# The last image's 3x3 convolution in a four-layer network: four output columns from six transformed parts, in blocks of 16 rows

## The chip, the cores and the metric

The kernel is one program on one core of a Trainium2 chip. The metric is the device time of one execution in microseconds, as the median of several runs. A profiled execution, which the hardware profiler records, is longer than the others; its own time and span stand in the table below.

## The reference

Four images of 256 channels and 64x64 pixels, in fp32, go through four layers, each of the form x = x + layer(groupnorm(x)). Layer 0 is a deformable convolution with a feed-forward part, layer 1 a linear attention with 5x5 depthwise convolutions, layer 3 an attention against a pooled image. The change is in layer 2, a 3x3 convolution with weights reduced to their sign times a scale for each output channel:

```python
def _L2_conv_ref(x, weights):                      # x: groupnorm of the image, 256 x 64 x 64
    real_w = weights.reshape(256, 256, 3, 3)
    scale = mean(abs(real_w), axis=(1, 2, 3), keepdims=True)
    bin_no_grad = scale * sign(real_w)
    clipped = clip(real_w, -1.0, 1.0)
    bin_w = (bin_no_grad - clipped) + clipped
    return conv2d(x, bin_w, stride=1, padding=1)
...
x = x + _L2_conv_ref(_gn(x), L2_conv_weights)      # 32 groups of 8 channels
x = x + _L3_conv_ref(_gn(x), ...)
```

## The kernel before

Channels lie on the 128 partitions in KT = 2 halves, pixels along the free dimension. The four images are staged one behind the other, and each stage runs the gathers of one image (`sample`, indirect DMAs issued by POOL) beside later layers of earlier images. Each layer is a generator that yields costs; `beside` (in `run`) advances several generators in proportion, so that their instructions interleave. Within `with ordered():` the order so emitted is the order on TensorE, VectorE (DVE), ScalarE (ACT) and GpSimd (POOL). The last call of `beside`, for the last image's layer 2 and the rest of the third image's layer 3 (`rest`), stands outside `ordered`; there the framework's scheduler decides the order of each engine from its own estimates, and that order is fixed in the program.

`binarise` runs once, beside the second image's `sample`, within the first fifth of it. It makes the weights' signs and scales and transforms each row of three taps into four, which `w2_d` holds in DRAM; its share of the interleaving is planned from the constant `BINARY`, 62.

`layer2` works in NB = 8 blocks of 8 rows. `normed` loads ten padded rows (`xp`, on the SP queue) and normalises them on ACT (L1048). `parts` makes, from each group of four neighbouring columns, four parts of two output columns (L1036; on POOL for the last two images, where `self.alone` is set, on DVE before). For each output half m and each pair of parts, twelve matmuls with 256 columns (two parts, two input halves, three row taps, L1085) sum into one PSUM bank. `leave` (L1061 on) adds the bank to the block's pixels `xv`: the first pair is the output columns themselves (L1065), the second a shared sum and difference (L1067 to L1069). The statistics of layer 3's groupnorm (`stats`, L110) and the store to `x5_d` (L1072) follow. `leave` is called through the list `before`, during the matmuls of the next bank; banks of the last image come from `long`, which cycles through the tags `acc` and `dp`. The next block's `normed` and `parts` are called in the middle of the current block.

At the start of the last stage, the last image's layer 1 ends (its matmuls to L943, its store at L954). The four attention steps of a block in the third image's layer 3 are each scores (L1185), maximum (L1186), exp (L1191), transpose (L1197) with its copy (L1199), and product (L1203); a block ends with L1213. After the last image's layer 2, only its layer 3 is left (`pooled(N - 1, True)`).

```python
CONV, SECOND = NB * 22.5 + 11, 568
...
beside(range(STEPS), STEPS, (conv(N - 1, "right"), CONV, 0, 1), (rest, 150, 0, 1))
```

Of the kernel before, what the change touches and what calls it, by code (L numbers as in the profile page):

```python
# [9 lines left out]
F32 = mybir.dt.float32  # L10
I32 = mybir.dt.int32
AF = mybir.ActivationFunctionType
ALU = mybir.AluOpType
# [4 lines left out]
P = 128  # L18
N, C, H, W = 4, 256, 64, 64
HW = H * W  # L20
KT = C // P
NB = HW // 512
# [4 lines left out]
NCH = NT // CT  # L27
# [9 lines left out]

CONVOLVE, OFFSETS, BINARY = NB * 9 + 26, 60, 62  # L40
FEED = NB * 40 + 8
LINEAR, LAST = 938, 624
STEPS = 900
CONV, SECOND = NB * 22.5 + 11, 568
EPS_BN = 1e-5
EPS_GN = 1e-5
EPS_ATT = 1e-5
# [24 lines left out]
class Net:  # L72
# [131 lines left out]
    def setup(self):  # L204
        nc, cp, a = self.nc, self.cp, self.a
# [38 lines left out]
        dt = self.dp.tile  # L244
# [5 lines left out]

        self.s_d = [dt([HW * PT, G * 5], F32, name=f"sd{n}") for n in im]
        self.w2_d = dt([P, KT, 3, 4, C], F32, name="w2")

    def binarise(self):


        nc = self.nc
        parts = [(k, slice(t, t + 3)) for k in range(KT) for t in range(0, 9, 3)]
        with self.tc.tile_pool(name="bin", bufs=1, side="left") as sp, \
                self.tc.tile_pool(name="bin2", bufs=2, side="left") as bp:  # L260

            def real(part):
                k, t = part
                w = bp.tile([P, 3, C], F32, name="w")
                nc.sync.dma_start(w, self.a["w2T"][:, k, t])
                return w

            sums = sp.tile([P, 6, C], F32, name="sums")
            for i, part in enumerate(parts):
                w = real(part)  # L270
                yield 1
                t = bp.tile([P, 3, C], F32, name="t")
                nc.vector.scalar_tensor_tensor(t, w, -1.0, w, ALU.mult, ALU.max)
                nc.vector.tensor_reduce(sums[:, i], t.rearrange("p t o -> p o t"), AX.X, ALU.add)
                yield 2
            ps = self.ps()
            for i in range(6):
                nc.tensor.matmul(ps[:, 0:C], self.ones, sums[:, i], start=i == 0, stop=i == 5)
            scale = sp.tile([P, C], F32, name="scale")
            nc.scalar.activation(scale, ps[:, 0:C], AF.Copy, scale=1.0 / (C * 9))  # L280
            yield 2
            for part in parts:
                w = real(part)
                yield 1
                t = bp.tile([P, 3, C], F32, name="t")
                s = bp.tile([P, 3, C], F32, name="s")
                nc.vector.tensor_scalar(t, w, 0.0, None, ALU.is_lt)
                nc.vector.scalar_tensor_tensor(s, w, 0.0, t, ALU.is_gt, ALU.subtract)
                nc.vector.tensor_tensor(s, s, scale.unsqueeze(1).to_broadcast([P, 3, C]), ALU.mult)
                yield 3  # L290
                nc.vector.tensor_scalar(t, w, -1.0, 1.0, ALU.max, ALU.min)
                nc.vector.tensor_tensor(s, s, t, ALU.subtract)
                nc.vector.tensor_tensor(s, s, t, ALU.add)
                yield 2
                u = bp.tile([P, 4, C], F32, name="u")
                nc.scalar.copy(u[:, 0], s[:, 0])
                nc.scalar.activation(u[:, 1], s[:, 2], AF.Copy, scale=-1.0)
                nc.scalar.activation(t[:, 0], s[:, 1], AF.Copy, scale=0.5)
                nc.vector.tensor_tensor(t[:, 1], s[:, 0], s[:, 2], ALU.add)
                for e, op in ((2, ALU.add), (3, ALU.subtract)):  # L300
                    nc.vector.scalar_tensor_tensor(u[:, e], t[:, 1], 0.5, t[:, 0], ALU.mult, op)
                nc.sync.dma_start(self.w2_d[:, part[0], part[1].start // 3], u)
                yield 2


# [791 lines left out]
            before.pop()()  # L1097


    def layer3(self, n, st, wide=False):  # L1100
        nc, tc, a = self.nc, self.tc, self.a
        M = HW // 4
        with tc.tile_pool(name=f"na{n}", bufs=1, side="left") as sp, \
# [17 lines left out]
            ps = self.ps()  # L1121
# [96 lines left out]
    def run(self):  # L1218
# [15 lines left out]
        def beside(steps, number, *works):  # L1234


            spent, open_ = [0] * len(works), set(range(len(works)))

            def advance(share):
                for j in sorted(open_):  # L1240
                    work, total, lo, hi = works[j]
                    while j in open_ and lo <= share and spent[j] < total * (share - lo) / (hi - lo) or share >= hi:
                        cost = next(work, None)
                        if cost is None:
                            open_.discard(j)
                        if not cost:
                            break
                        spent[j] += cost

            for i, _ in enumerate(steps, 1):  # L1250
                advance(i / number)
            while any(works[j][3] <= 1 for j in open_):
                advance(1)
# [28 lines left out]
        with ordered():  # L1282
            beside(range(STEPS), STEPS, (feed(N - 1), FEED, 0, 0.27), (linear(N - 1), LAST, 0.27, 1), (rest, SECOND, 0.27, 1.05))
        self.spare = False
        beside(range(STEPS), STEPS, (conv(N - 1, "right"), CONV, 0, 1), (rest, 150, 0, 1))

        self.banks = cycle(["mm", "mm", "mm", "vk"])
        for _ in pooled(N - 1, True):
# [95 lines left out]
```

## Time and profile before

| what | value |
|---|---|
| time, median of 3 runs | 7713.78 us (7711.9 to 7732.44) |
| profiled execution, own time | 8695.07 us |
| span of the profiled execution | 8693.3 us |
| mean granted TensorE clock | 0.803 |
| busy over the span: PE, PE weight load | 5880.0 us (68%), 3498.6 us (40%) |
| busy over the span: DVE, ACT, POOL | 4817.7 us (55%), 3541.0 us (41%), 4934.7 us (57%) |
| first and last gather issued by POOL | 137.1 us, 7190.2 us |
| last image's layer 2: first record of L1085, last one's start | 8306.88 us, 8481.8 us |

"Busy" is the time in which an engine executes; PE is TensorE's matmuls, "PE weight load" its loads of stationary operands, which overlap matmuls. A line such as `L1085 PE MATMUL ps<-xd,w` is the code's line, the engine, the operation and its output and inputs by the program's names. Every matmul in fp32 appears as two records. In lists in order of time, the first number is the start in microseconds from the span's start and the second a length; what stands in brackets is the idle time before it and what ended it.

### The profile page before, as it was taken

The page shows a single profiled execution, that of the slowest core. Times are in us where ns is not written, and L with a number is a line of the kernel's source. Part 1 is how long each engine was busy: PE and PEld are TensorE (multiplying, and loading weights), DVE is VectorE, ACT ScalarE, POOL GpSimd, SP SyncE. Part 2 cuts the span into 40 slices and gives each one's busy share as a digit, 9 for nine tenths or more (in the row PEclk, how much of TensorE's full clock was granted, in tenths as well). Part 3 has the DMA queues.
Part 4 walks back from the last instruction along what each step waited for, and adds up shares of the span by engine and source line. Part 5 has one row for each costly group of instructions (what it writes and reads, how often), then busy time and mean ns, then how long its engine had stood idle before and what let it go on. Part 6 is the DMA issues. An engine that isn't in the chain of part 4 may idle for free.

```text
span 8693.3 us, 99761 instructions
## 1 busy us (share of the span) xinstructions
PE 5880.0 (68%) x35776; PEld 3498.6 (40%) x35776; DVE 4817.7 (55%) x6045; ACT 3541.0 (41%) x10767; POOL 4934.7 (57%) x4870
## 2 busy tenths in 40 slices
PE   4454554448744446688876676888766778986899
PEld 2232222224323222234644443345544333664476
DVE  5344442443366667324776675228766762699833
ACT  2333333234444433334445443444454442456414
POOL 2666666466666666666666556666655560476410
PEclk7676766669866667799988887999878879998899
DMA  6454554444533334444543344445433342220131
GB/s 172 129 160 123 145 149 118 114 143 148 158 107 106 110 109 126 137 127 138 142 133 111 111 116 138 146 135 142 141 105 111 112 118 96 74 72 29 44 97 54
DMA packets 744383, 1031.75 MB, mean 119 GB/s; under 512 B 354128, under 2 KB 459984, under 8 KB 742352
## 3 DMA queue, kind: packets, MB, share of 16 engines
q0 software_dynamic: 221184, 604.27, 24.4%
q1 hardware_dynamic: 522704, 421.10, 16.4%
q8 instruction: 283, 4.64, 0.2%
q14 instruction: 212, 1.74, 0.1%
HBM read 856.39 MB, written 168.61 MB: 118 GB/s over the span
## 4 chain that ended last, share of the span: by engine, by line
PE 43%; another core or an unknown queue 17%; DVE 17%; ACT 13%; issue 8%; DMA 1%; POOL 0%; SPq 0%; ACTq 0%; DVEq 0%; POOLq 0%
DVE agg L178 10%; PE acc L603 6%; PE ps L739 5%; PE ps L749 5%; ACT wm L588 5%; PE ps L1085 4%; PE ps L821 3%; PE ps L943 2%; PE ps L1203 2%; PE s L1185 2%; PE po L636 2%; ACT dT L623 2%; ACT at L608 1%; PE rden L934 1%
## 5 line engine op out<-in xcount | busy, mean ns | idle before, releaser
L596 POOL DMA_INDIRECT g<-tab,sl x4608 | 4399.0, 955 | 2790.8 <-issue 1179.7
L178 DVE SCALAR_TENSOR_TENSOR agg<-pad,vec,agg 128x1024 f32<-128x1024 f32 x2280 | 2934.5, 1287 | 63.9
L603 PE MATMUL acc<-g,wm 128*32 128x128 f32 x18432 | 1012.4, 336 | 2022.6 <-ACT at L608 1471.8
L603 PEld LDWEIGHTS acc<-g,wm 128*32 128x32 f32 x18432 | 557.7, 129 | 2524.7 <-ACT at L608 1683.4
L588 ACT ACTIVATE wm<-sl,con 128x48 f32<-128x48 f32 x6144 | 1490.1, 366 | 26.0 <-remote 12.6
L1085 PE MATMUL ps<-xd,w 128*128 128x256 f32 x3072 | 741.0, 392 | 37.6 <-issue 30.1
L623 ACT COPY dT<-dp 64x128 f32<-64x128 f32 x1152 | 297.2, 258 | 985.8 <-remote 524.3
L1085 PEld LDWEIGHTS ps<-xd,w 128*128 128x128 f32 x3072 | 587.3, 196 | 159.0 <-issue 79.0
L739 PE MATMUL ps<-x2f,f 128*128 128x512 f32 x1024 | 502.3, 639 | 10.2 <-issue 5.1
L608 ACT COPY at<-acc 128x256 f32<-128x256 f32 x576 | 214.5, 372 | 712.8 <-remote 607.4
L821 PE MATMUL ps<-xr,qw 128*128 128x512 f32 x768 | 463.5, 733 | 21.8 <-issue 8.5
L724 DVE SCALAR_TENSOR_TENSOR hm<-ps,vec,lk 128x512 f32<-128x512 f32 x256 | 190.6, 750 | 502.4 <-ACT lk L741 375.2
L749 PE MATMUL ps<-hm,f 128*128 128x512 f32 x1024 | 463.6, 601 | 0.0
L741 ACT ACTIVATE lk<-ps,low 128x512 f32<-128x512 f32 x256 | 174.0, 687 | 514.7 <-PE ps L739 413.2
L636 PE MATMUL po<-dT,ow 128*128 128x288 f32 x1024 | 336.7, 477 | 56.5 <-issue 13.8
L875 ACT COPY kt<-pt 128x512 f32<-128x512 f32 x256 | 149.5, 585 | 544.8 <-remote 246.8
L1036 POOL TENSOR_TENSOR xd<-xp 128x640 f32<-128x640 f32 x64 | 79.8, 1275 | 497.3 <-DMA xq<-x 280.3
L1203 PE MATMUL ps<-gt,pT 128*128 128x129 f32 x2048 | 316.5, 315 | 47.1 <-ACT pT L1199 32.9
L613 PE MATMUL dp<-ident,at 128*128 128x128 f32 x1152 | 285.5, 336 | 77.1 <-ACT dT L623 53.4
L1203 PEld LDWEIGHTS ps<-gt,pT 128*128 128x128 f32 x2048 | 297.2, 226 | 98.8 <-ACT pT L1199 45.0
L1185 PE MATMUL s<-ph,th 128*128 128x512 f32 x512 | 289.2, 677 | 42.9 <-DVE ot L938 9.2
L739 PEld LDWEIGHTS ps<-x2f,f 128*128 128x128 f32 x1024 | 199.2, 203 | 253.3 <-issue 238.5
(243 smaller groups left out, 7710.6 us busy)
## 6 DMA issues: line engine op xcount, KB each, us to landing
g<-tab,sl POOLq DMA_INDIRECT x4608
x<-x SPq DMA_DIRECT2D x128, 512.0 KB
xr<-x SPq DMA_DIRECT2D x96, 512.0 KB
tab<-xo SPq DMA_DIRECT2D x192, 128.0 KB
x<-in_x SPq DMA_DIRECT2D x32, 512.0 KB
y<-yc SPq DMA_DIRECT2D x32, 512.0 KB
yb<-y SPq DMA_DIRECT2D x64, 256.0 KB
x<-yb SPq DMA_DIRECT2D x64, 256.0 KB
```

The lines of the kernel that those rows point to most:

```text
L178: nc.vector.scalar_tensor_tensor(to, s, wt, acc, ALU.mult, ALU.add)
L588: nc.scalar.activation(wm[:, :, :, o], blocks[b][:, r:r + WR, G:], AF.Copy, scale=self.con("own")[:, o:o + 1])
L596: nc.gpsimd.indirect_dma_start(out=g[:, i, :], out_offset=None, in_=table, in_offset=bass.IndirectOffsetOnAxis(ap=sl.bitcast(I32)[:, r, i: ...
L603: nc.tensor.matmul(acc[32 * i:32 * i + 32, :], wm[:, r4, 4 * i + 2 * x:4 * i + 2 * x + 2, :], g[:, i, x * P:(x + 1) * P], start=x == 0, st ...
L623: nc.scalar.copy(dT[b][hs, :, r:r + UR], dp[u][hs, :, :, s, :].rearrange("p v g o -> p g v o"))
L636: nc.tensor.matmul(po[m][:, 0:BR * OB], self.ow[:, k, m * P:(m + 1) * P], dT[b][:, k].rearrange("p r o -> p (r o)"), start=k == 0, stop=k ...
L739: nc.tensor.matmul(ps, f1[:, k, m * P:(m + 1) * P], x2[:, k], start=k == 0, stop=k == KT - 1)
L749: nc.tensor.matmul(ps, f2[:, k, m * P:(m + 1) * P], hm[:, k], start=k == 0, stop=k == 4 * KT - 1)
L821: nc.tensor.matmul(ps, qw[:, k, m * P:(m + 1) * P], x[:, k], start=k == 0, stop=k == KT - 1)
L1085: nc.tensor.matmul(ps[:, e], w[:, k, t, 2 * half + e, m * P:(m + 1) * P], v[:, 2 * half + e, k, t:t + 8], start=i % 6 == 0, stop=i % 6 == 5)
L1185: nc.tensor.matmul(s[i], tv[:, 4 * b + j], ph[:, i * 512:(i + 1) * 512], start=True, stop=True)
L1203: nc.tensor.matmul(ps[:, 0:P + 1], pT[:, m], gt[:, m], start=m == 0, stop=m == 7)
```

## The change

The last image takes a new function, `layer2_fours`, in place of `layer2`; the other three keep `layer2`. It works in NCH = 4 blocks of 16 rows. Six columns give six parts of four output columns, made as three pairs `va`, `vb`, `vc`; the first block's parts are made on DVE, those of later blocks on DVE and POOL. Each pair is twelve matmuls with 256 columns (16 rows of 16 column groups), into one bank of now three (`acc`, `dp`, `vk`). The drains become three kinds, one for each pair, with copies on ACT (L1181, L1183) and sums on DVE. The weights have six transformed taps in `w4_d`, which `binarise` makes beside the four; they are loaded in six DMAs into three tiles. The input of the first block and its padding are asked for ahead of the groupnorm. `BINARY` becomes 86 and `CONV` 150.

```diff
@@ -37,11 +37,11 @@
 
 
 
-CONVOLVE, OFFSETS, BINARY = NB * 9 + 26, 60, 62
+CONVOLVE, OFFSETS, BINARY = NB * 9 + 26, 60, 86
 FEED = NB * 40 + 8
 LINEAR, LAST = 938, 624
 STEPS = 900
-CONV, SECOND = NB * 22.5 + 11, 568
+CONV, SECOND = 150, 568
 EPS_BN = 1e-5
 EPS_GN = 1e-5
 EPS_ATT = 1e-5
@@ -250,6 +250,7 @@
 
         self.s_d = [dt([HW * PT, G * 5], F32, name=f"sd{n}") for n in im]
         self.w2_d = dt([P, KT, 3, 4, C], F32, name="w2")
+        self.w4_d = dt([P, KT, 3, 6, C], F32, name="w4")
 
     def binarise(self):
 
@@ -301,6 +302,20 @@
                     nc.vector.scalar_tensor_tensor(u[:, e], t[:, 1], 0.5, t[:, 0], ALU.mult, op)
                 nc.sync.dma_start(self.w2_d[:, part[0], part[1].start // 3], u)
                 yield 2
+                u = bp.tile([P, 6, C], F32, name="u4")
+                q = bp.tile([P, 2, C], F32, name="q")
+                nc.scalar.activation(q[:, 0], s[:, 1], AF.Copy, scale=1 / 6)
+                nc.scalar.activation(q[:, 1], s[:, 1], AF.Copy, scale=1 / 12)
+                nc.vector.scalar_tensor_tensor(t[:, 2], s[:, 0], 0.25, s[:, 2], ALU.mult, ALU.add)
+                for e, op in ((0, ALU.subtract), (1, ALU.add)):
+                    nc.vector.scalar_tensor_tensor(u[:, e], t[:, 1], -1 / 6, q[:, 0], ALU.mult, op)
+                yield 2
+                for e, op in ((2, ALU.add), (3, ALU.subtract)):
+                    nc.vector.scalar_tensor_tensor(u[:, e], t[:, 2], 1 / 6, q[:, 1], ALU.mult, op)
+                nc.scalar.activation(u[:, 4], s[:, 0], AF.Copy, scale=0.25)
+                nc.scalar.copy(u[:, 5], s[:, 2])
+                nc.sync.dma_start(self.w4_d[:, part[0], part[1].start // 3], u)
+                yield 2
 
 
     def weights(self, pool):
@@ -1094,6 +1109,119 @@
                                         d = next(ahead)
                                 yield 1.4
                         before.append(partial(leave, b, m, half, ps, xv))
+            before.pop()()
+
+
+    def layer2_fours(self, n, st, st3):
+
+
+        nc, tc = self.nc, self.tc
+        R, V = 16, W // 4
+        with tc.tile_pool(name=f"ca{n}", bufs=1, side="right") as sp, \
+                tc.tile_pool(name=f"cb{n}", bufs=2, side="right") as bp:
+            w = [sp.tile([P, KT, 3, 2, C], F32, name=f"w{e}") for e in range(3)]
+            for e in range(3):
+                for k in range(KT):
+                    nc.sync.dma_start(w[e][:, k], self.w4_d[:, k, :, 2 * e:2 * e + 2])
+            stt, tt = nc.vector.scalar_tensor_tensor, nc.vector.tensor_tensor
+
+            def loaded(c):
+
+                lo, hi = max(R * c - 1, 0), min(R * c + R + 1, H)
+                xp = bp.tile([P, KT, R + 2, W + 4], F32, name="xp")
+                for v in [xp[:, :, :, 0:1], xp[:, :, :, W + 1:]] + [xp[:, :, 0:1, 1:W + 1]] * (c == 0) \
+                        + [xp[:, :, R + 1:, 1:W + 1]] * (c == NCH - 1):
+                    nc.vector.memset(v, 0.0)
+                inner = [xp[:, k, lo - R * c + 1:hi - R * c + 1, 1:W + 1] for k in range(KT)]
+                for k in range(KT):
+                    nc.sync.dma_start(inner[k], self.x4_d[n][:, k, lo * W:hi * W].rearrange("p (r w) -> p r w", w=W))
+                return xp, inner
+
+            def normed(inner):
+                for k in range(KT):
+                    nc.scalar.activation(inner[k], inner[k], AF.Identity, bias=bi[:, k:k + 1], scale=sc[:, k:k + 1])
+
+            def parts(xp, add):
+
+                d = xp.rearrange("p k r (x d) -> p k r x d", d=4)
+                col = lambda i: d[:, :, :, i // 4:i // 4 + V, i % 4]
+                two = lambda i: d[:, :, :, i // 4:i // 4 + V, i % 4:i % 4 + 2].rearrange("p k r x d -> p d (k r) x")
+                new = lambda name, **more: bp.tile([P, 2, KT, R + 2, V], F32, name=name, **more)
+                flat = lambda v: v.rearrange("p d k r x -> p d (k r) x")
+                pq, a = new("pq", bufs=1), new("va")
+                stt(pq[:, 0], col(2), -4.0, col(4), ALU.mult, ALU.add)
+                stt(pq[:, 1], col(1), -4.0, col(3), ALU.mult, ALU.add)
+                add(a[:, 0], pq[:, 0], pq[:, 1], ALU.add)
+                add(a[:, 1], pq[:, 0], pq[:, 1], ALU.subtract)
+                yield a
+                r, u, a = new("pr", bufs=1), new("pu", bufs=1), new("vb")
+                add(flat(r), two(4), two(2), ALU.subtract)
+                add(flat(u), two(2), two(0), ALU.subtract)
+                yield
+                stt(a[:, 0], u[:, 1], 2.0, r[:, 0], ALU.mult, ALU.add)
+                stt(a[:, 1], u[:, 1], -2.0, r[:, 0], ALU.mult, ALU.add)
+                yield a
+                a = new("vc")
+                stt(a, u, -4.0, r, ALU.mult, ALU.add)
+                yield a
+
+            def leave(c, m, e, ps, xv):
+
+                y = xv[:, m].rearrange("p (q a b) -> p a b q", a=2, b=2)
+                if e == 2:
+                    for i in range(2):
+                        tt(y[:, i, i], y[:, i, i], ps[:, i], ALU.add)
+                    for h in range(2):
+                        nc.vector.bn_stats(st3[:, m, 2 * c + h, :], xv[:, m, h * 512:(h + 1) * 512])
+                    if m == KT - 1:
+                        nc.sync.dma_start(self.x5_d[n][:, :, c * 1024:(c + 1) * 1024], xv)
+                    return
+                f = bp.tile([P, 2, 256], F32, name="f")
+                o = bp.tile([P, 2, 256], F32, name="o")
+                nc.scalar.copy(f[:, 0], ps[:, 0])
+                if e:
+                    nc.scalar.activation(f[:, 1], ps[:, 0], AF.Copy, scale=2.0)
+                tt(o[:, 0], ps[:, 1], f[:, 0], ALU.add)
+                stt(o[:, 1], ps[:, 1], -2.0 if e else -1.0, f[:, e], ALU.mult, ALU.add)
+                if e:
+                    tt(y[:, 0], y[:, 0], o, ALU.add)
+                    stt(y[:, 1], o, 4.0, y[:, 1], ALU.mult, ALU.add)
+                else:
+                    tt(y, y, o.unsqueeze(1).to_broadcast([P, 2, 2, 256]), ALU.add)
+
+            xp, inner = loaded(0)
+            sc, bi = yield from self.groupnorm(sp, st, "g2")
+            normed(inner)
+            v = []
+            for a in parts(xp, tt):
+                v += [a] if a is not None else []
+                yield 2
+            before = []
+            for c in range(NCH):
+                xv = bp.tile([P, KT, 1024], F32, name="x4")
+                nc.sync.dma_start(xv, self.x4_d[n][:, :, c * 1024:(c + 1) * 1024])
+                now, v, ahead = v, [], None
+                for m in range(KT):
+                    for e in range(3):
+                        ps = self.long().rearrange("p (e q) -> p e q", e=2)
+                        for i in range(12):
+                            j, k, t = i // 6, i // 3 % 2, i % 3
+                            nc.tensor.matmul(ps[:, j], w[e][:, k, t, j, m * P:(m + 1) * P], now[e][:, j, k, t:t + R],
+                                             start=i % 6 == 0, stop=i % 6 == 5)
+                            if i % 3 == 2:
+                                if before and i > 5:
+                                    before.pop()()
+                                if i == 5 and c + 1 < NCH:
+                                    if not (m or e):
+                                        xp, inner = loaded(c + 1)
+                                    elif not m and e == 1:
+                                        normed(inner)
+                                        ahead = parts(xp, nc.gpsimd.tensor_tensor)
+                                    else:
+                                        a = next(ahead)
+                                        v += [a] if a is not None else []
+                                yield 1.4
+                        before.append(partial(leave, c, m, e, ps, xv))
             before.pop()()
 
 
@@ -1282,7 +1410,9 @@
         with ordered():
             beside(range(STEPS), STEPS, (feed(N - 1), FEED, 0, 0.27), (linear(N - 1), LAST, 0.27, 1), (rest, SECOND, 0.27, 1.05))
         self.spare = False
-        beside(range(STEPS), STEPS, (conv(N - 1, "right"), CONV, 0, 1), (rest, 150, 0, 1))
+        self.idle = cycle(["acc", "dp", "vk"])
+        fours = self.layer2_fours(N - 1, st[2][1], st[3][1])
+        beside(range(STEPS), STEPS, (fours, CONV, 0, 1), (rest, 150, 0, 1))
 
         self.banks = cycle(["mm", "mm", "mm", "vk"])
         for _ in pooled(N - 1, True):
```

## The prediction

> **What bounds the kernel now.** I began with the page's engine totals and slices, went from there to the busy times by stretch to find the stage that the edit touches, then to the groups of that stage, then to TensorE's instructions in order of time at its start, and last to the chain and the waits. Columns of the stretches: from:to, length, then busy time and number of instructions for PE, weight load, DVE, ACT and POOL, the granted TensorE clock, the DMA share and GB/s.
>
> ```profile
> 2000.00:2300.00 300.00, 257.00 (x1319) 118.50 (x1317) 101.19 (x154) 124.67 (x413) 190.08 (x195) 0.95 0.47 139
> ...
> 8272.00:8307.00 35.00, 26.71 (x99) 19.17 (x98) 12.24 (x35) 14.72 (x23) 3.82 (x4) 0.76 0.56 182
> 8307.00:8482.30 175.30, 174.84 (x825) 152.69 (x823) 51.09 (x107) 20.89 (x27) 36.07 (x29) 1.00 0.28 80
> ```
>
> The third line is the last image's convolution: TensorE is busy 174.84 of 175.30 us at full clock, while DVE, ACT and POOL are busy 51, 21 and 36 us. So TensorE alone sets this stage. The groups of 8283 to 8490 us say what it does:
>
> ```profile
> L1085 PE MATMUL ps<-xd,w 128*128 128x256 f32 x768 | 167.2, 379 | 0.0
> ...
> L1036 POOL TENSOR_TENSOR xd<-xp 128x640 f32<-128x640 f32 x32 | 39.9, 1280 | 210.3 <-PE ps L1203 107.4 <-PE ps L1085 96.4 <-ACT xp L1048 6.4
> L110 DVE BATCH_NORM_STATS2 st<-x 128x6 f32<-128x512 f32 x16 | 11.1, 694 | 0.5
> L1048 ACT ACTIVATE xp<-xp,g_bi,g_r 128x640 f32<-128x640 f32 x12 | 11.1, 923 | 71.9 <-DMA xp<-x 71.9
> ...
> L1068 DVE TENSOR_TENSOR x<-x,ps 128x256 f32<-128x256 f32 x16 | 6.8, 422 | 0.5
> ```
>
> Each matmul in the code is two records here (384 in the code, 768 in the trace). A record's 379 ns overlaps its neighbour's; the pace is read from the chain:
>
> ```profile
> 8341.88 5.18 PE ps L1085 x24
> 8348.78 133.40 PE ps L1085 x618
> ```
>
> 133.40 / 618 = 0.2159 us a record. The other stretch that matters is the start, where TensorE's order reads
>
> ```profile
> 8283.36 1.88 PE L1185 MATMUL s<-ph,th 128*128 128x512 f32 x4
> ...
> 8293.41 2.74 PE L1185 MATMUL s<-ph,th 128*128 128x512 f32 x4
> 8299.25 1.97 PE L1197 MATMUL pt<-ident,pe 128*128 128x128 f32 x8 [3.10 <-ACT pe L1191]
> 8301.09 2.09 PE L1203 MATMUL ps<-gt,pT 128*128 128x129 f32 x8
> 8302.97 1.91 PE L1185 MATMUL s<-ph,th 128*128 128x512 f32 x2
> 8304.68 1.39 PE L1203 MATMUL ps<-gt,pT 128*128 128x129 f32 x8
> 8305.91 1.13 PE L1185 MATMUL s<-ph,th 128*128 128x512 f32 x2
> ```
>
> These are the last attention steps of the image before (scores s, maximum, exp, transpose, product), one dependent chain per step, about 10 us each with TensorE half idle. The third and fourth of the block's four steps stand between convolution matmuls, which fill their gaps: convolution starts at 8306.88 and ends at 8482.2.
>
> [...] sixteen L1203 records take 3.79 us at 8289.83, after idling, and 1.95 us elsewhere. [...] the trace has 422 ns for 256 and 690 ns for 512, so I use it for 576 (0.76 us) and 1152 (1.36 us). [...] the old parts step 8 bytes (1280 ns for 640, 2.0 ns each), the new ones 16, which the trace doesn't show. [...]
>
> **The change, part by part.**
>
> *Matmuls.* 4 blocks x 2 halves x 3 pairs x 12 = 288 in the code, 576 records instead of 768, of the same 128x256 shape from packed operands. 192 x 0.2159 = 41.5 us less on the path; 576 x 0.2159 = 124.4 us remain.
>
> *The start.* The built order of TensorE puts all four attention steps ahead of the first convolution matmul; two of them stood among convolution work before. Only the block's four L1213 records (1.9 us) are still inside. From the rows above: a step without the 1.28 us table load that the second one has takes 5.84 - 1.28 us from scores to transpose, 1.84 to the product, and 3.5 for the product's sixteen records at half clock, 9.9 us. The third then starts at 8301.09 + 2.09 + 1.39, about 8304.6, the fourth at 8314.5, and convolution at 8324.4. With TensorE warm a step is 3.63 + 1.33 + 1.95 = 6.9 us, so 8318.4 is the other end. I take 9.4 a step, 8323.4[...]. End of convolution: 8323.4 + 124.4 + 1.9 = 8449.7, against 8482.2: 32.5 us gained. Of the 41.5, 9 go back because two steps have lost their cover.
>
> *What must be there at 8323.4.* Weights: 4.7 MB in six DMAs instead of 3.1 MB in one. SP issued the old load at 8280.1; the 6.3 MB up to and with the first input block, at about 330 GB/s (the slices after it show 367 and 309), land by about 8300. The x4 block and second input block follow. Normalisation (L1048's successor) is queued on ACT after the third step's pT copies, so it waits for nothing, and two such of about 1.4 us delay no exp. On DVE the first parts (two of 576, one of 1152, two of 576: 4.4 us) come after the fourth step's maximum, at about 8318.3, and are ready at 8322.7. Hidden by 0.7 us; if 16-byte steps double DVE's time, it costs 3 to 4 us.
>
> *DVE, ACT, POOL beside the matmuls.* A block is 144 records, 31.1 us. DVE: per half 0.42 x 6 + 0.69 x 2 + 1.22 for the 1024-element add + 0.69 x 2, 6.5 us; twice is 13.0, and the parts add 1.5 + 1.5 + 1.36, 17.4 in all, 70 us for the stage against 51, under 124. ACT: two normalisations of 1.4 and six copies of 0.4, 5.2 us a block. [...] All are covered.
>
> *New waits.* Three PSUM banks rotate instead of two, so a bank's drain has 10.4 us. In front of bank 1's drain DVE now waits for POOL's differences of the next block; bank 3's copy stands on ACT behind the normalisation of the fourth input block, whose DMA waits for the second block's parts. [...] bounds 0 and 6 us, taken 1.
>
> *End.* The last drain (two adds and two statistics, 2.2 us) is as long as the old one (0.69 + 0.42 + 0.42 + 0.69); the last store is 1 MB instead of 0.5 MB, read 10 us later: nothing.
>
> *Weight preparation.* Outside the last stage only `binarise` differs in the order of any engine: 24 more ACT instructions (about 0.41 us as L296, 9.8 us) and 30 on DVE (0.42 as L301, 12.7 us), six more stores on SP ahead of some loads, all by 2300 us in the second image's sampling. There DVE is busy 101 of 300 us and ACT 125; gathers run at 0.65 per us as they do after 2300 (269 in 400). Cost between 0 and 22.5 us if all of it lay on the gather's loop. POOL waits for TensorE there for only a small part, but TensorE is busy 86%. I take 3.
>
> *Sum.* -32.5 + 1 + 3 = -28.5 us. The profiled span goes from 8693.3 to 8664.8, its execution from 8695.07 to about 8666.6. The runs' median, 7713.78, is 981 us below that execution; the last stage has no gathers and TensorE is at its pace, so I subtract the same amount: 7685.3 us.
>
> **Rivals.**
> - *Cover stays* (0.18): TensorE stays warm through the attention steps and nothing stalls. 8318.8 as start (DVE's parts then set it), 37.1 gained, preparation at 0: 7676.7. [...] Against: the 3.79 and 2.74 us rows.
> - *Drains fall behind* (0.18): the POOL and ACT waits above cost 4 us in each of the three blocks that prepare a successor: 28.5 - 11 = 17.5 gained, 7696. [...] Against: DVE is 44% idle.
> - *Preparation on the gather's loop, ending slower* (0.12): the 22.5 us lie on the path, and DVE waits for ACT's scaled copies as L301 did for L298 and L297 (17.2 us for its twelve instructions). 22.5 + 17.2 = 39.7 against 31.5 gained: 7722. It decides when over four fifths of that is exposed. For: ACT's `at` copies hold up L603, and TensorE is 86% busy. Against: POOL's rate is no lower in this stretch.
> - That the change doesn't do what it says is excluded by the built order, which has 288 matmuls.
>
> **How the numbers follow.** The likeliest case (7685.3) has 0.52. About 0.3% (23 us) is what a measurement can tell from no change: the line is 7690.6. Faster: all of the second case, four fifths of the likeliest, little of the third: 0.62. Slower by over 23 us needs the last case and more: 0.06. The same: 0.32. The range, 7667 to 7709, takes in the full 41.5 with a few us of removed idling below, and above the drains' 6 us more plus a part of the preparation; the last case's upper part is left out.
>
> **What would show it.** Right: 576 convolution records at 0.216 us; first one near 8323, last near 8450, less than 2 us idle between; four attention steps ahead of it at 9 to 10 us. Wrong: gaps before every third bank with POOL or ACT as releaser (third case); a start later than 8328, or weights as its releaser; the gathers after 2300 us shifted by over 10 us (last case).

## The result, and the profile after

| what | kernel before | changed kernel |
|---|---|---|
| time, median of 5 runs each, side by side | 7718.1 us (7711.9 to 7732.44) | 7686.32 us (7682.92 to 7689.01) |
| ratio, with 95% interval | | 0.9957 (0.9942 to 0.9971) |
| profiled execution: own time, span | 8695.07, 8693.3 us | 7685.26, 7683.5 us |
| first scores of the third image's last block to the last convolution record's start | 198.4 us | 162.9 us |
| of it, ahead of the first convolution record | 23.5 us | 33.9 us |
| of it, from the first convolution record to the last one's start | 174.9 us | 129.0 us |
| from there to the end of the span | 211.5 us | 212.8 us |

The change saves 31.8 us; the interval of the ratio makes that 22 to 45 us. In some sets of runs the unchanged kernel takes some 7718 us, in others some 8757 us (the shown profile of before, at 8695.07 us, is of this longer kind), and the profiles part ahead of the last stage (last gather issued at 7190.2 us in that of before, at 6233.8 us in that of after), so times are compared within a set only. Between sets only stretches of the last stage are compared: what was traced in both agrees (from the last convolution record's start to the end 211.5 to 213.3 us in all twelve traces; from the block's first scores to the convolution 33.9 us in every trace with the changed kernel's start). Two traces of the same kernel can differ by 3 us there, as the changed kernel's second run below shows.

The stretches of the changed kernel's attention steps and convolution (from and to, length, busy time and instructions of PE, weight load, DVE, ACT and POOL, granted clock, DMA share, GB/s):

```profile
7290.00:7341.80 51.80, 39.47 (x169) 27.68 (x167) 20.27 (x49) 21.78 (x34) 0.00 (x0) 0.90 0.71 207
7341.80:7470.80 129.00, 126.98 (x580) 109.81 (x580) 99.39 (x118) 18.88 (x34) 28.59 (x12) 1.00 0.27 79
```

TensorE is still busy nearly throughout (126.98 of 129.00 us). But DVE, third of the busy times, is no longer an engine with much to spare: 99.39 us, where the prediction had 70. TensorE's instructions in order of time at the stage's start, and two later banks:

```profile
7307.85 1.88 PE L1313 MATMUL s<-ph,th 128*128 128x512 f32 x4
...
7316.50 2.07 PE L1313 MATMUL s<-ph,th 128*128 128x512 f32 x4
7321.66 1.23 PE L1325 MATMUL pt<-ident,pe 128*128 128x128 f32 x8 [3.09 <-ACT pe L1319]
7323.05 3.69 PE L1331 MATMUL ps<-gt,pT 128*128 128x129 f32 x16 [0.15 <-ACT pT L1327]
7326.57 1.98 PE L1313 MATMUL s<-ph,th 128*128 128x512 f32 x4
7330.37 1.24 PE L1325 MATMUL pt<-ident,pe 128*128 128x128 f32 x8 [1.81 <-ACT pe L1319]
7331.75 2.06 PE L1331 MATMUL ps<-gt,pT 128*128 128x129 f32 x16
7333.65 1.98 PE L1313 MATMUL s<-ph,th 128*128 128x512 f32 x4
...
7341.78 5.45 PE L1209 MATMUL ps<-va,w 128*128 128x256 f32 x24 [0.89 <-DVE va L1154]
...
7387.37 5.34 PE L1209 MATMUL ps<-vc,w 128*128 128x256 f32 x24
7392.55 5.34 PE L1209 MATMUL ps<-va,w 128*128 128x256 f32 x24
```

As the prediction said, four attention steps stand ahead of the convolution. The second lasts from 7316.50 to 7326.57, 10.1 us, with its sixteen product records at the slow pace (3.69 us); the third lasts 7.1 us, with the same sixteen records in 2.06 us. A bank of 24 records takes 7392.55 - 7387.37 = 5.18 us, 0.2158 us a record: the pace of before. TensorE's waits in the stage, by what released it (us in total, times, longest):

```profile
PE ps L1209 <- DVE o L1185: 1.0, 1, 1.0
PE ps L1209 <- DVE x L1173: 1.0, 2, 0.5
PE ps L1209 <- DVE va L1154: 0.9, 1, 0.9
```

The first two lines are waits for a bank whose drain was late; the third is the first block's parts, in the stretch ahead of the convolution.

### The profile page after: what moved, and what is told of

Same layout as the page of the kernel before. It is cut to its first block, busy times and chain, and to the rows that moved or that the text cites. A ratio compares the mean times of both kernels' runs of the same rounds, so it can differ in the third digit from the quotient of the medians.

```text
span 7683.5 us, 99438 instructions
## 1 busy us (share of the span) xinstructions
PE 5885.2 (77%) x35584; PEld 3437.1 (45%) x35584; DVE 4876.2 (63%) x6099; ACT 3543.5 (46%) x10807; POOL 4927.6 (64%) x4850
## 4 chain that ended last, share of the span: by engine, by line
PE 36%; DVE 21%; POOL 6%; ACT 6%; issue 6%; DMA 3%; SPq 0%; DVEq 0%; POOLq 0%; ACTq 0%
DVE agg L178 14%; PE ps L754 6%; POOL g L611 6%; PE ps L764 6%; PE acc L618 4%; PE ps L836 3%; PE ps L1331 2%; PE s L1313 2%; PE ps L958 2%; PE ps L1100 2%; PE po L651 2%; DMA g<-tab,sl 2%; DVE mx L1314 1%; PE pt L1325 1%; PE ps L1209 1%
## 5 line engine op out<-in xcount | busy, mean ns | idle before, releaser
L618 PE MATMUL acc<-g,wm 128*32 128x128 f32 x18432 | 1287.0, 325 | 1245.1 <-ACT at L623 739.3
L618 PEld LDWEIGHTS acc<-g,wm 128*32 128x32 f32 x18432 | 634.9, 123 | 1949.7 <-ACT at L623 976.3
L1100 PE MATMUL ps<-xd,w 128*128 128x256 f32 x2304 | 546.4, 386 | 6.0 <-DVE x L1084 3.4
L754 PE MATMUL ps<-x2f,f 128*128 128x512 f32 x1024 | 479.6, 616 | 4.0 <-ACT f L729 4.0
L1100 PEld LDWEIGHTS ps<-xd,w 128*128 128x128 f32 x2304 | 431.9, 194 | 89.1 <-issue 33.2
L651 PE MATMUL po<-dT,ow 128*128 128x288 f32 x1024 | 303.9, 445 | 28.7 <-ACT dT L646 12.5
L200 POOL TENSOR_TENSOR ak<-ak,m 128x1024 f32<-128x1024 f32 x96 | 227.8, 2373 | 120.2 <-ACT m L196 115.8
```

What stands on the lines that cost most here:

```text
L618: nc.tensor.matmul(acc[32 * i:32 * i + 32, :], wm[:, r4, 4 * i + 2 * x:4 * i + 2 * x + 2, :], g[:, i, x * P:(x + 1) * P], start=x == 0, st ...
L651: nc.tensor.matmul(po[m][:, 0:BR * OB], self.ow[:, k, m * P:(m + 1) * P], dT[b][:, k].rearrange("p r o -> p (r o)"), start=k == 0, stop=k ...
L754: nc.tensor.matmul(ps, f1[:, k, m * P:(m + 1) * P], x2[:, k], start=k == 0, stop=k == KT - 1)
L1100: nc.tensor.matmul(ps[:, e], w[:, k, t, 2 * half + e, m * P:(m + 1) * P], v[:, 2 * half + e, k, t:t + 8], start=i % 6 == 0, stop=i % 6 == 5)
```

## The experiments

My theory is the prediction's likeliest case: TensorE sets this stage, so a matmul record less is its 0.216 us less (0.2158 in the changed kernel's trace, as above); some microseconds come back because attention steps lose their cover; drains and parts are hidden; the weight preparation costs next to nothing. The rivals are the preparation on the gather's path and drains that fall behind. Four kernels ran in a set in which the kernel before takes 8757.08 us, four in one with 7717.62 us, two in one with 7721.06 us. The changed kernel itself was run again in the second set only; the kernels of the other sets are compared with the kernel before beside them.

### The kernel before, again

No edit.

> The kernel before, unchanged, run once more, as a control of the comparison and for a second profile. Every theory expects a ratio of 1.000 within about 0.003. The first profile of this kernel spanned 8693.3 us with gathers to 7190.2 us, against 6233.8 us in the new kernel's profile. If that is the profile's own doing, the second span is near 7715 us with the last gather near 6235 to 6240 us; if it belongs to the kernel, the span is again near 8690 us. In both, the last image's convolution takes 768 records at 0.216 us and the stretch from the first scores of the third image's last block to the last convolution record is 198.8 us.

Measured: 8761.39 us against 8757.08 us, ratio 1.0005 (0.9993 to 1.0016). From the block's first scores to the last convolution record it takes 198.3 us, as in the profile shown. The interval of this difference of nothing runs from -6 to +14 us. The profiled execution took 8761.39 us, as the others did, so the length of the first profile was not the profiling's doing; nor is it the kernel's alone, which takes some 7718 us beside the changed one.

### The weight preparation alone

The kernel before, with `w4_d`, the preparation of six taps in `binarise`, and the new constant, but with its old convolution:

```diff
-CONVOLVE, OFFSETS, BINARY = NB * 9 + 26, 60, 62
+CONVOLVE, OFFSETS, BINARY = NB * 9 + 26, 60, 86
...
+        self.w4_d = dt([P, KT, 3, 6, C], F32, name="w4")
...
+                nc.scalar.activation(q[:, 0], s[:, 1], AF.Copy, scale=1 / 6)
...
+                nc.sync.dma_start(self.w4_d[:, part[0], part[1].start // 3], u)
```

> The kernel before with only the preparation of the six-tap weights added (BINARY 86); the last convolution stays as it was and nothing reads the new weights. Prediction's step: 3 us more, bounds 0 and 10 (7718 to 7728, ratio 1.000 to 1.0013). From the two traces: the last stage gained 35 to 36 us and the whole 31.8, which leaves about 4 us for this. Rival, preparation on the gather's loop: up to 39.7 us more, 7758, ratio 1.005.

Measured: 8756.01 us, ratio 0.9998 (0.9986 to 1.0009), so -12 to +8 us. The rival of 39.7 us falls, and 22.5 us with it; a cost of 3 us can't be told from none. DVE's new instructions do wait for ACT, as that rival had it (9.2 us in two waits at L311 in this trace, 16.7 us in five in the changed kernel's). So the wait is there, and no cost of it shows in the time. That holds for this set, in which the gathers take longer; the preparation alone was not run where the kernel before takes some 7718 us.

### Sixteen matmuls a bank

The changed kernel with the middle of the three row taps multiplied twice, so that 768 records come back (its convolution is not the reference's):

```diff
-                            nc.tensor.matmul(ps[:, j], w[e][:, k, t, j, m * P:(m + 1) * P], now[e][:, j, k, t:t + R],
-                                             start=i % 6 == 0, stop=i % 6 == 5)
+                            for again in range(1 + (i % 3 == 1)):
+                                nc.tensor.matmul(ps[:, j], w[e][:, k, t, j, m * P:(m + 1) * P], now[e][:, j, k, t:t + R],
+                                                 start=i % 6 == 0, stop=i % 6 == 5)
```

> The new kernel with 16 matmuls for each bank in place of 12 (the tap in the middle row is added twice, so the last image's convolution is not the reference's): 768 records again, everything else as in the new kernel. If TensorE alone sets the stage, 192 x 0.2159 = 41.5 us come back less the 2.5 us of waits that a longer bank time hides: the time is 39 to 41.5 us above the new kernel, near 7726, ratio to before about 1.001. If the drains on DVE and ACT set the stage (rival), the added matmuls hide in part and it rises by less than 20 us, to 7706 or below.

Measured: 8758.16 us, ratio to the kernel before 0.9999 (0.9989 to 1.0009): the gain is gone. Its convolution's records, with the shortest, median and longest (ns) and the first and last start:

```profile
L1210 PE MATMUL ps<-va,w x256: 379/379/483, 8364.2 to 8517.8; 128*128 128x256 f32 x128
L1210 PE MATMUL ps<-vc,w x256: 379/379/379, 8378.1 to 8531.6; 128*128 128x256 f32 x128
```

From the first start to the last that is 167.4 us, 38.4 more than the changed kernel's 129.0 and 41.3 more than the second run of it below (126.0); 192 x 0.2159 is 41.5. No wait of TensorE is left in it but the 0.9 us for the first parts. From the first scores to the last record it takes 201.3 us, 3.0 us more than the kernel before again (198.3): with as many matmuls and no drain in the way, about 3 us is what the new order of the start costs.

### The first input ahead of the weights

The loads of the weights go behind the first block's; the framework's scheduler then puts the third and fourth attention steps back between convolution matmuls:

```diff
-            for e in range(3):
-                for k in range(KT):
-                    nc.sync.dma_start(w[e][:, k], self.w4_d[:, k, :, 2 * e:2 * e + 2])
...
             xp, inner = loaded(0)
+            for e in range(3):
+                for k in range(KT):
+                    nc.sync.dma_start(w[e][:, k], self.w4_d[:, k, :, 2 * e:2 * e + 2])
```

> The new kernel with the first block's input asked for ahead of the weights on SP. The scheduler then puts three of the attention steps' parts among convolution matmuls again. Theory of lost cover: TensorE idles 6.3 us between the second step's transpose and the first convolution record in the new kernel; most of it is filled, and the stretch from the first scores of the last block to the last convolution record falls from 163.3 us to about 158, the time by 5 us to 7681 (ratio to before 0.9952). Rival, the weights (4.7 MB, now later) or DVE's parts end last instead: convolution starts earlier but waits, and the time is 7686 or above.

Measured: 8709.69 us, ratio to the kernel before 0.9950 (0.9936 to 0.9965). The order in time on TensorE:

```profile
8366.58 5.34 PE L1209 MATMUL ps<-va,w 128*128 128x256 f32 x24
8371.76 1.46 PE L1209 MATMUL ps<-vb,w 128*128 128x256 f32 x6
8373.14 1.24 PE L1325 MATMUL pt<-ident,pe 128*128 128x128 f32 x8
8374.21 0.60 PE L1209 MATMUL ps<-vb,w 128*128 128x256 f32 x2
8374.65 1.95 PE L1331 MATMUL ps<-gt,pT 128*128 128x129 f32 x16
```

The transpose and product of the third step now lie inside a bank, without a wait. From the first scores to the last record it takes 160.3 us, where I expected 158. Against the changed kernel's first trace (162.9) that is 2.6 us less, against its second (159.9) nothing. New waits took a part: 2.2 us of the second step's product for its copy on ACT, and 2.0 us of L1341 for its input `m` from ACT (L1336). That covering the steps again is worth little fits with the 3 us that uncovering them cost. The time is 47 us (31 to 56) below the kernel before in this set, and the 38 us by which the stretch is shorter lie within that.

### The changed kernel, again

No edit; it is the control for the times of three of the next five kernels and, for its trace, for all.

> The changed kernel again, as the control for the three kernels beside it. Every theory: 0.4 to 0.5% less than the kernel before on the same chip where the kernel before takes about 7715 us, or where it takes about 8757 us some 0.3 to 0.5% less (30 to 36 us); in the trace the convolution takes 129 us from its first matmul's start to its last one's, and the stretch from the block's first scores to the last convolution matmul 163 us.

Measured: 7683.83 us against 7717.62, ratio 0.9960 (0.9946 to 0.9973), 33.8 us. From first scores to last record 159.9 us, 33.9 of them ahead of the convolution and 126.0 in it. That is 576 records (124.4 us) and four L1341 records (1.7 us) with no gap: the three waits for drains, in the first trace 2.0 us and about 2.9 with what follows them, did not occur in this execution. So the drains are just in time in one execution and just late in another.

### Two banks in rotation

```diff
-        self.idle = cycle(["acc", "dp", "vk"])
+        self.idle = cycle(["acc", "dp"])
```

> The changed kernel with two PSUM banks in rotation in place of three. Theory (the drains are long now, and the third bank is what hides them): a bank of 5.2 us of matmuls is followed by a drain that begins only in the next bank's matmuls and lasted up to 20 us after its sums in the blocks that prepare a successor (bank 1's sums of the first block ended about 6 us after the matmuls of bank 3 began). With two banks TensorE waits for drains by VectorE and ScalarE, 6 to 10 us in all, and the time is 6 to 10 us above the changed kernel beside it. Rival (VectorE has slack enough, the third bank is not needed): stalls below 1 us, time within 2 us of the changed kernel.

Measured: 7691.56 us, 7.7 above the control. The order on TensorE:

```profile
7353.76 5.34 PE L1209 MATMUL ps<-vc,w 128*128 128x256 f32 x24
7364.62 6.27 PE L1209 MATMUL ps<-va,w 128*128 128x256 f32 x18 [5.52 <-ACT xp L1142]
```

The size is as the theory had it, the distribution is not: it is one wait, of 5.5 us, and the 18 records after it take 6.27 us in place of the control's 4.05, a slower pace after the wait. Together 7.7 us. The releaser named is a normalisation on ACT, which doesn't touch this bank. The bank's readers are the copies L1181 and L1183 on ACT (done at 7354.6) and the sums L1184 and L1185 on DVE, the last of which ends at 7364.48; I take that one to be the releaser; the profile does not name it. Its place in DVE's queue was behind a first part of 3.42 us and a wait of 2.2 us for POOL.

### All parts on VectorE

```diff
-                                        ahead = parts(xp, nc.gpsimd.tensor_tensor)
+                                        ahead = parts(xp, tt)
```

> The changed kernel with all parts made on VectorE, GpSimd idle in this stage. Theory (a GpSimd operation and a VectorE operation that read SBUF hold each other up, which is why a first part takes 1.75 us on average and up to 3.3 us beside GpSimd where it takes 1.19 us alone): L1152 and L1153 fall to 1.1 to 1.25 us each in all four blocks, VectorE's busy time in the convolution stays at 95 to 108 us although it does more, TensorE waits less than 1.5 us, and the time is that of the changed kernel within 2 us. Rival (the 16-byte step alone makes them slow, and GpSimd's help is real): L1152 and L1153 stay near 1.75 us, VectorE is busy 115 us or more, waits of TensorE rise to 5 us or more and the time with them.

Measured: 7688.02 us, 4.2 above the control's median where I had allowed 2, but inside the control's spread (7680.25 to 7690.81), and with a ratio of 0.9959 against 0.9960. First the changed kernel's first trace, DVE and then POOL in order of time:

```profile
7350.43 3.40 DVE L1152 SCALAR_TENSOR_TENSOR pq<-xp 128x576 f32<-128x576 f32 x1
7353.75 3.37 DVE L1153 SCALAR_TENSOR_TENSOR pq<-xp 128x576 f32<-128x576 f32 x1
```

```profile
7349.03 3.70 POOL L1158 TENSOR_TENSOR pr<-xp 128x1152 f32<-128x1152 f32 x1 [128.79 <-DMA xp<-x]
7352.69 3.36 POOL L1159 TENSOR_TENSOR pu<-xp 128x1152 f32<-128x1152 f32 x1
```

And the same lines by number, shortest, median and longest (ns), with all parts on DVE:

```profile
L1152 DVE SCALAR_TENSOR_TENSOR pq<-xp x4: 1189/1196/1221, 7338.8 to 7384.2; 128x576 f32<-128x576 f32 x4
L1187 DVE TENSOR_TENSOR x<-x,o x8: 1072/1099/1133, 7361.4 to 7469.5; 128x512 f32<-128x512 f32 x8
L1190 DVE TENSOR_TENSOR x<-x,o x8: 1985/2036/2075, 7350.7 to 7464.0; 128x1024 f32<-128x1024 f32 x8
```

The same part takes 3.4 us beside POOL and 1.2 us without it, and with POOL idle none takes more than 1.22 us. Beside POOL each of the two ends 1.1 us after a POOL operation has ended, as if it had waited for that and then run. POOL's L1158, too, took 3.70 us here and 2.42 us in the next block. How little POOL's help is worth shows in DVE's busy time (the third of the busy times), in the control and with all parts on DVE:

```profile
7340.30:7466.40 126.10, 126.10 (x580) 110.03 (x580) 97.30 (x118) 18.88 (x34) 30.86 (x12) 1.00 0.27 81
7344.00:7472.50 128.50, 126.24 (x579) 109.87 (x580) 101.52 (x130) 18.85 (x34) 0.00 (x0) 1.00 0.27 80
```

The moved operations of three blocks are 3 x (2 x 2.26 + 2 x 0.75) = 18.1 us of work for DVE, and 4.2 us is all that it is busier. Giving them to POOL thus relieved DVE by less than a quarter of their work. TensorE's waits for drains were 2.3 us here, 2.1 of them for L1185, over the 1.5 that I had allowed. The stretch from first scores to last record is 162.6 us, between the changed kernel's own two traces (162.9 and 159.9). So the theory that the two hold each other up, called the lock from here on, fits what was measured; whether the time is "the same within 2 us" these runs can't tell.

### Input first, and all parts on VectorE

Both edits together.

> The changed kernel with the first block's input asked for ahead of the weights, and all parts on VectorE. If the two attention steps again find cover between convolution matmuls, the stretch from the block's first scores to the last convolution matmul takes 158 to 161 us where the changed kernel takes 163, and the time is 2 to 5 us below the changed kernel beside it. If the waits for the interleaved attention steps (4 us with the input first alone) come from VectorE's longer queue, it is no better than the changed kernel, 0 to 2 us.

Measured: 7682.74 us, 1.1 below the control, which is less than either's spread and short of the 2 to 5 us expected; from first scores to last record 158.3 us against 159.9. ACT's 2.2 us wait of the second step is there again, and 1.7 us for a drain (L1182 in this kernel, the changed kernel's L1185). It is the shortest stretch of all, but not a faster kernel by what these runs can tell.

### Two banks, and all parts on VectorE

Both edits together.

> Two PSUM banks in rotation and all parts on VectorE, GpSimd idle in this stage. The two banks alone gave one wait of 5.5 us: the fourth bank of the first block needed the second one's drain, which stood on VectorE behind first parts of 3.4 us beside GpSimd and behind a wait of 2.2 us for GpSimd. Theory (GpSimd's part in it, the lock and the wait, made the drain late): that wait is gone or below 1 us, because with the parts on VectorE the same drain ended at 7359.3, 0.4 us before the fourth bank was due; the convolution takes 127 to 130 us from its first matmul's start to its last one's, against 133.9 us with two banks and GpSimd. Rival (the drains and parts are simply too long for two banks): waits of 4 to 8 us, 131 to 135 us.

Measured: 7693.11 us, and 133.8 us of convolution, as with two banks and POOL. Order on TensorE, at the place of the old wait and in the block after it:

```profile
7367.79 4.05 PE L1209 MATMUL ps<-va,w 128*128 128x256 f32 x18
...
7382.84 5.42 PE L1209 MATMUL ps<-vc,w 128*128 128x256 f32 x24 [2.82 <-DVE o L1185]
7389.86 5.42 PE L1209 MATMUL ps<-va,w 128*128 128x256 f32 x24 [1.60 <-DVE o L1185]
```

The wait of the fourth bank is gone, as the theory says, so that one came with POOL's work. But at the first block's last bank and the second block's first three, waits of 2.8, 1.6, 0.45 and 2.1 us come in its place, all for DVE, and the total is the rival's. With two banks the drains come too late, with POOL or without; the third bank is worth 5 to 8 us (133.8 us of convolution against 128.7 with three banks and the parts on DVE, 7.7 us of time in the pair above).

### Drains to adjoining pixels

```diff
-                y = xv[:, m].rearrange("p (q a b) -> p a b q", a=2, b=2)
+                y = xv[:, m].rearrange("p (a b q) -> p a b q", a=2, b=2)
```

> The changed kernel with each drain adding to 256 adjoining pixels in place of every fourth one (the output columns land in the wrong pixels; the amount of work is the same). Theory (the step of four pixels, 16 bytes, is what makes the drains long): the 1024-element sum L1190 falls from 2.2 us to 1.2 to 1.4 us, the 512-element ones L1187 and L1188 from 1.3 to 1.5 us to 0.7 to 0.9 us, VectorE's busy time in the convolution from 97 to 99 us to 80 to 87 us; TensorE sets the stage, so the time is that of the changed kernel or up to 2 us below. Rival (the lock with GpSimd is what makes them long): they stay above 1.8 us and 1.1 us.

Measured: 7683.38 us against 7721.06 before in the same set, ratio 0.9955 (0.9942 to 0.9969), as the changed kernel (0.9960 and 0.9957 in its sets). The drains, in the control and then here:

```profile
L1187 DVE TENSOR_TENSOR x<-x,o x8: 1076/1100/2384, 7359.0 to 7463.1; 128x512 f32<-128x512 f32 x8
L1190 DVE TENSOR_TENSOR x<-x,o x8: 2033/2054/2895, 7347.0 to 7457.6; 128x1024 f32<-128x1024 f32 x8
...
L1187 DVE TENSOR_TENSOR x<-x,o x8: 682/693/2694, 7358.8 to 7461.1; 128x512 f32<-128x512 f32 x8
L1190 DVE TENSOR_TENSOR x<-x,o x8: 1224/1226/2980, 7345.1 to 7455.6; 128x1024 f32<-128x1024 f32 x8
```

The medians fall from 1.10 to 0.69 us and from 2.05 to 1.23 us: these are within 0.01 us the prices that the prediction had used (0.69 and 1.22). The means (1.11 and 1.57 us) do not fall as far as I expected, since single instances beside POOL take 2.7 and 3.0 us. So both causes are there: the step of 16 bytes makes every drain 0.4 to 0.8 us longer, the lock a few of them by 2 us. DVE is busy 84.0 us in place of 97.3, and no drain holds TensorE up. The time stays where it was, since in the control none did either.

## Why the prediction was right, step by step

The time of 7685.3 us was right, and so was the mechanism of the gain: TensorE sets the stage, and a matmul less is its pace less. What was wrong lies beside it, above all DVE's load. Term by term, with the first profile of the changed kernel (and the second where it differs), in microseconds:

| step | predicted | measured |
|---|---|---|
| matmuls | -41.5 | -41.3 (sixteen a bank against the second run) |
| two attention steps lose their cover | +9 | +3.2 |
| new waits in the convolution | +1 | +2.9 (0 in the second run) |
| weight preparation | +3 | between -12 and +8 |
| end | 0 | +1.3 (stretch after the last record; 211.5 to 213.3 over all twelve traces) |
| stage, first scores to last record | -31.5 | -35.5 (-38.5) |
| whole | -28.5 | -31.8 (-33.8) |

*Matmuls.* Right, in number, pace and worth. The 41.5 us came off the path because TensorE set the old stage at 174.84 of 175.30 us, and at 126.98 of 129.00 us still sets the new one.

*The start.* The mechanism was right, its size wrong by 6.1 us: 40.0 us from the first scores to the convolution were predicted, 33.9 came. The first two steps took 18.7 us for 21.2. In the kernel before, L129 waited 0.93 us for DVE ahead of the first step's product, the second step's scores ran slower (2.74 us for 2.07), and a piece of the convolution's normalisation (0.87 us) stood between that step's two copies on ACT; in the changed kernel L129 comes after the product and the normalisation after the third step's copies. The third and fourth took 15.2 us with the wait for the parts, for 18.8: "I take 9.4 a step", an estimate between 9.9 and 6.9, was the wrong choice; they ran at 7.1 us, near the 6.9. Both paces are in the trace: sixteen records took 3.69 us where the granted clock was 0.55 (7323.00 to 7326.80), and 2.06 us where it was 1.00 (7331.70 to 7333.90). In the trace of before it was 0.50 over the row of 3.79 us (8289.80 to 8293.70); this and 1.00 are the prediction's "half clock" and "warm". The length of the gap alone doesn't tell which holds: the block's first step has a gap of 1.75 us ahead of its transpose and runs slow (3.66 us), the third has 1.81 us and runs fast. Ahead of these gaps TensorE had worked 6.9 us with one break of 0.15 us before the third step, 3.7 us before the first. Whether that is the reason was not tried. Nor does a longer wait always slow what follows. In the second run of the kernel before, 18 records took 5.74 us in place of 4.05 soon after a wait of 2.0 us:

```profile
8388.44 1.16 PE L1203 MATMUL ps<-gt,pT 128*128 128x129 f32 x8 [2.04 <-ACT pT L1199]
8389.44 5.74 PE L1085 MATMUL ps<-xd,w 128*128 128x256 f32 x18
```

But with two banks and all parts on DVE, 24 records right after a wait of 2.8 us took 5.42 us in place of 5.34. The lost cover is then 33.9 - 23.5, less the 7.2 us of the two steps' own work that left the convolution (174.9 - 165.8 - 1.9): 3.2 us, for which sixteen matmuls a bank gave 3.0 independently.

*The first parts* "hidden by 0.7 us; if 16-byte steps double DVE's time, it costs 3 to 4 us". Those with such steps did cost more (1.2 us for 576, 2.3 for 1152, against 0.76 and 1.36), and 0.9 us of wait came of it, not 3 to 4: two of the five operations ahead of the convolution (L1154, L1155) read and write adjoining elements and stayed at 0.78 us, and the first matmul waited for L1154 alone. No wait of TensorE was for the weights.

*DVE beside the matmuls.* Here the working failed: 70 us were predicted, 99.4 came. The step that failed is the use of the price of before's drains, which step 8 bytes (422 ns for 256 elements, 690 for 512, and the straight line through the two), for operands that step 16; the lock with POOL stood in this sum at nothing. The differences to the groups of the trace account for it: L1190 17.8 - 9.8 us, L1187 and L1188 22.9 - 11.0, L1173 16 x (0.617 - 0.42), L1152 and L1153 of three blocks 11.6 - 4.6, together 30 us for the 29. With all parts on DVE, and so no lock, the same operations exceed the prediction by 19 us; these are the step, and the other 11 are put down to the lock. Drains to adjoining pixels confirm the first: their medians, 1226 ns for 1024 elements and 693 for 512, are within 3 ns of that line (1226 and 690).

*New waits.* "Bounds 0 and 6 us, taken 1", an estimate of mine that no row of before showed, held at 0 to 2.9. The lock shows in the changed kernel's trace, where it adds up to 2.2 us to a 1.2 us part (3.40 us at 7350.43, 1.19 at 7336.52). The rival of drains that fall behind wanted 12 us of waits. With three banks 0 to 2.9 came; with two the time was 7.7 us longer. DVE was 23% idle and not 44.

*POOL.* At the 2.0 ns an element of before's L1036, the 3456 elements of a block would take 6.9 us; 28.6 / 3 = 9.5 us came, with what it was held up beside DVE. The shortest difference of 1152 elements took 2.42 us, 2.1 ns an element, though its operands step 16 bytes.

*The offset.* I subtracted 981 us from the profiled execution of before as if a profiled execution were longer, as is also said with the metric. It isn't: that of after took 7685.26 us, among its runs, and so it is with every kernel here but the shown one of before, which stands among other runs, as told with the result. The subtraction did no harm because what it stood for lies ahead of the last stage, where no gain was forecast.

So the time came out within 1 us partly by luck. The start was 6 us better and the preparation perhaps 3 us, the waits were 1.9 us worse and the end perhaps 1.3 us. The sum was also set against a median of 7713.78 us, where the five runs beside the changed kernel have 7718.1: a gain 3.3 us larger than forecast and a time of before 4.3 us higher all but cancelled. And about 4 to 5 us between the stage's gain and that of the medians (35.5 and 31.8, 38.5 and 33.8) lie within the spread of the runs and were not traced. That is also about what the preparation was priced at, so a cost of that size is not excluded.

## What to carry to other kernels

Here one engine was busy through a stage at a constant pace, and removed instructions times that pace were the gain, less what the new order at the stage's edges uncovered. In such a stage those edges are the thing to work out. Price a strided DVE operand from a row with that very step (at 16 bytes 2.04 us here, 1.23 for adjoining elements), and do not count work moved to POOL as taken from DVE: here, where both worked on the same block's parts, three quarters of it came back as longer DVE instructions. One more bank in rotation was worth 5 to 8 us here, where DVE was busy 30 us longer over the stage than planned.

## What the runs showed of the hardware that was not expected

- An fp32 DVE operation whose operand steps 16 bytes took about 1.6 times as long as one with adjoining elements: 2.04 against 1.23 us for 1024 elements, 1.10 against 0.69 for 512.
- A DVE operation of 1.2 us beside a POOL operation took up to 3.4 us, ending 1.1 us after a POOL operation's end; with all parts on DVE and three banks none of the four was over 1.22 us.
- After a wait of 5.5 us TensorE's next 18 matmul records took 6.27 us in place of 4.05; the granted clock of that stage was 0.97, and 1.00 with three banks. After one of 2.8 us the next 24 took 5.42 us in place of 5.34.
